# Layer-3 blocks among layer-2 values, and the eigenvectors' end moved to the end of the scores

## Chip, cores and metric

The kernel runs on one core of one Trainium2 chip. The metric is the time of one execution on the device, in microseconds (us). Before the change the median of three runs is 2519.87 us (2519.52 to 2521.8).

## The reference

The input x holds 128 graphs of 64 nodes with 256 features in float32; all graphs share one 64 x 64 adjacency matrix. Four layers follow one another, each as `x = layernorm(x + layer(x))`:

- Layer 0: two graph convolutions with relu, then four LSTMs over windows of 1, 2, 3 and 4 nodes.
- Layer 1: a normalized graph convolution with two linear maps and batch norms.
- Layer 2: attention over 512 edges with 4 heads. Scores of edges, a softmax over the edges that share a source node, a weighted sum of the values, an output map.
- Layer 3: the eigenvectors of the graph's Laplacian as a basis.

```python
# layer 2 (src, dst: the edges; A0 the adjacency)
e = einsum('behd,hd->beh', leaky_relu(Xq[:, src] + Xq[:, dst], 0.2), a)
e = e + log(A0[src, dst] + EPS)
attn = softmax of e over the edges of one src
Y = segment_sum(attn * Xv[:, dst], src);  return Y @ W_out.T
# layer 3
_, U = eigh(L_norm)
h = relu(einsum('mn,bnd->bmd', U.T, x) @ W1 + b1)
return einsum('nm,bmd->bnd', U, h @ W2 + b2)
```

## The kernel before

Two graphs make 128 partitions, so x is a tile X of 128 partitions x 64 tiles x 256 features that stays in SBUF through all layers. Each layer works on its tiles in turn. A norm (`Norm`, line 1218) adds a layer's result to X (line 1231), takes statistics of each tile (1234, 1235), and for a group of tiles forms the inverse root (`inv_sqrt`, line 1206) and rescales X on ScalarE (1252).

**The eigenvectors** depend on the adjacency alone. Their computation (`FastEigh.steps`) is a generator named `pieces`, a long chain of small VectorE operations with a few TensorE products. `pump(n)` issues pieces worth n units of work between the instructions of other layers. Its last part, the merge to 64, finds each eigenvalue by 31 bisection steps (mid, den, its reciprocal, a dot product, a comparison), and then builds the vectors. In before.py what is left of it is issued by `for _ in pieces` at the start of layer 3 (line 2021). Then `again` is computed and read into a register, and a loop of 0 or 1 turns (line 2030) runs a general method if the fast one failed. For these inputs it is not entered. After it, bdu and bdut (two copies of U and of its transpose on the diagonal) are filled.

**Layer 2** is a set of generators, advanced by `run(...)` in an order written out by hand (lines 1982 to 1998):

- `scores` (line 1848), 32 steps of one pair of tiles: transposes of X (1830), maps to queries and values (1841), a store of the values to DRAM (xv, 1845), then in two parts the edge sums (l, 1864), a copy and a leaky relu (xs, 1870 and 1871) and the products with the head vector (sc, 1817). Steps 0 to 15 are half 0, 16 to 31 half 1. Each step ends with `pump(work[0])`.
- `softmax` of a half (line 1885): scans over sorted edges, on VectorE and ScalarE.
- `table` (1905) transposes a half's weights and scatters them by edge into a DRAM table (attn_d) with four indirect DMAs on GpSimd's queue. `fetch` (1920) reads the table back as dense matrices M2 by eight DMAs of 512 KB on SP's queue; each is cut into pieces of 64 floats, since a half has two M2 tiles of 64 columns.
- `values` (1955), 33 steps: `load` copies eight columns of M2 into mc (ScalarE, 1934) and fetches xr (GpSimd's queue, 1937), `mixed` multiplies them (1949) and copies the product to yT (1952, one half of it on VectorE, one on ScalarE), and one step later the output map (1971) goes into the norm.

In the hand-written order four values steps run among the scores of half 1; after the scores come the rest of the values, with softmax, table and fetch of half 1 among them.

**Layer 3** follows in blocks of four tiles, each in four stages that are one block apart: `basis` (2059), `first_map` (2069), `back` (2077), `second_map` (2086), the norm and the store to the output. GpSimd adds a constant to X (2063).

The Tile scheduler sets each engine's final order from the program's order and estimated times, and may move an instruction ahead of earlier ones on its engine, even ahead of the loop; every engine then takes its own queue in order.

Of the kernel before, what the change touches and what calls it, by code (L numbers as in the profile page):

```python
# [7 lines left out]
F32 = mybir.dt.float32  # L8
I32 = mybir.dt.int32
AF = mybir.ActivationFunctionType  # L10
# [1195 lines left out]
def inv_sqrt(nc, pool, o, h):  # L1206

    s = pool.tile(list(h.shape), F32, tag="is_s", name="is_s")
    r = pool.tile(list(h.shape), F32, tag="is_r", name="is_r")
    nc.scalar.activation(s, h, AF.Sqrt)  # L1210
    nc.vector.reciprocal(r, s)  # L1211
    nc.vector.tensor_tensor(r, r, h, ALU.mult)
    nc.vector.tensor_tensor(r, r, s, ALU.add)
    nc.vector.reciprocal(r, r)
    nc.vector.tensor_scalar(o, r, 2.0, None, ALU.mult)


class Norm:
# [21 lines left out]
    def flush(self):  # L1240
        nc, n = self.nc, len(self.todo)
        v = self.pool.tile([P, self.n], F32, tag="ln_v", name="ln_v")
        rs = self.pool.tile([P, self.n], F32, tag="ln_rs", name="ln_rs")
        nc.vector.tensor_scalar(v[:, :n], self.mv[:, :n, 1], 1e-5, None, ALU.add)  # L1244
        inv_sqrt(nc, self.pool, rs[:, :n], v[:, :n])
        if self.act:
            sh = self.pool.tile([P, self.n], F32, tag="ln_sh", name="ln_sh")
            nc.vector.scalar_tensor_tensor(sh[:, :n], self.mv[:, :n, 0], -1.0, rs[:, :n], ALU.mult, ALU.mult)  # L1248
        for k, t in enumerate(self.todo):
            x = self.X[:, t, :]  # L1250
            if self.act:
                nc.scalar.activation(x, x, AF.Identity, bias=sh[:, k : k + 1], scale=rs[:, k : k + 1])  # L1252
                continue
            nc.vector.tensor_scalar(x, x, self.mv[:, k, 0:1], rs[:, k : k + 1], ALU.subtract, ALU.mult)
        self.todo = []
# [3 lines left out]
def tile_adj_resnorm(ctx: ExitStack, tc: tile.TileContext, I: dict, out: bass.AP, layers: int = 4):  # L1259
# [45 lines left out]
    bdu = const.tile([P, P], F32, tag="bdu", name="bdu")  # L1305
    bdut = const.tile([P, P], F32, tag="bdut", name="bdut")
# [7 lines left out]
    def col(tag):  # L1314
        return ek.tile([P, 1], F32, tag=tag, name=tag)
# [4 lines left out]
    cs_, deg, dg, jk = col("cs_"), col("deg"), col("dg"), ek.tile([P, P], F32, tag="jk", name="jk")  # L1320
# [8 lines left out]
    deg1, dinv, dv = col("deg1"), col("dinv"), ek.tile([P, P], F32, tag="dv_", name="dv_")  # L1329
# [19 lines left out]
    v.scalar_tensor_tensor(A, A, dinv[:N], dr, ALU.mult, ALU.mult)  # L1349
    U = ek.tile([P, N], F32, tag="U", name="U")  # L1350
# [417 lines left out]
    with tc.tile_pool(name="l2w", bufs=1) as lw, tc.tile_pool(name="l2s", bufs=2) as sm, tc.tile_pool(  # L1768
        name="l2p", bufs=2, space=PSUM
    ) as pp, tc.tile_pool(name="l2g", bufs=2, space=PSUM) as pg, tc.tile_pool(  # L1770
        name="l2c", bufs=2, space=PSUM
    ) as pc, tc.tile_pool(name="l2d", bufs=1, space=bass.MemoryType.DRAM) as dl:
# [51 lines left out]
        def transposed(k):  # L1824

            xT = []
            for t in (2 * k, 2 * k + 1):
                ps = pp.tile([P, 512], F32, tag="m", name="m")
                for c in range(2):
                    te.transpose(ps[:, c * P : (c + 1) * P], X[:, t, c * P : (c + 1) * P], ident)  # L1830
                xT.append(sm.tile([P, 2, P], F32, tag="xT", name="xT"))
                v.tensor_copy(xT[-1].rearrange("p c n -> p (c n)"), ps[:, :D])  # L1832
            return xT

        def maps(k, xT):

            xq, xv = [], sm.tile([P, 2, D], F32, tag="xv", name="xv")
            for i in range(2):
                ps = pp.tile([P, 512], F32, tag="m", name="m")
                for c in range(2):  # L1840
                    te.matmul(ps, xT[i][:, c, :], wqv[:, c, :], start=(c == 0), stop=(c == 1))  # L1841
                xq.append(sm.tile([P, D], F32, tag="xq", name="xq", bufs=4))
                taken.append(s.copy(xq[i], ps[:, :D]))  # L1843
                s.copy(xv[:, i, :], ps[:, D:])
            nc.sync.dma_start(xvd[k], xv)
            return xq

        def scores():
# [8 lines left out]
            for k in range(K):  # L1857
                xn = None
                for c in range(2):
# [8 lines left out]
                    for b, i in four:  # L1868
                        x = xs[b, i] = sm.tile([P, E], F32, tag="xs", name="xs", bufs=7)
# [15 lines left out]
        def softmax(half, es):  # L1885
# [5 lines left out]
            for c, e in enumerate(es):  # L1891
                f = sm.tile([P, E], F32, tag="sf", name="sf", bufs=1)
# [12 lines left out]
        def table(es):  # L1905

            at = sm.tile([P, 4, 2, HU, 2, 4], F32, tag="at", name="at", bufs=1)
            pt = pg.tile([P, 2, 512], F32, tag="l", name="l")
            for c, e in enumerate(es):
                ps = pt[:, c, :]  # L1910
# [9 lines left out]
        def fetch(half):  # L1920

            M2[half] = [lw.tile([P, N, N], F32, tag="M2", name="M2", bufs=3) for _ in range(2)]
            for k in range(2):
                for n0 in range(0, N, 32):
                    for b in range(2):
                        q = b * P + k * N
                        nc.sync.dma_start(
                            M2[half][k][b * N : (b + 1) * N, n0 : n0 + 32, :],
                            attn_d[: N * N, q : q + N].rearrange("(d n) q -> d n q", n=N)[:, n0 : n0 + 32, :])

        def load(k):
# [3 lines left out]
                   M2[half][u_ // 8][:, :, u_ % 8 * 8 : u_ % 8 * 8 + 8].rearrange("p n q -> p q n"))  # L1935
            x = sm.tile([P, 2, D], F32, tag="xr", name="xr")
# [3 lines left out]
        def mixed(m, x):  # L1940

            yT = sm.tile([P, 2, 2, P], F32, tag="yT", name="yT")
            for b in range(2):
# [8 lines left out]
                (s.copy if b else v.tensor_copy)(yT[:, :, :, r], py[:, :D].rearrange("p (i c n) -> p i c n", i=2, c=2))  # L1952
            return yT

        def values():
# [3 lines left out]
            for k in range(K + 1):  # L1959
# [6 lines left out]
                if k:  # L1966
                    po = (pg.tile([P, 2, 512], F32, tag="l", name="l")[:, 0, :] if alone[0] else
                          pp.tile([P, 512], F32, tag="m", name="m"))
# [10 lines left out]
        alone = [False]  # L1979
# [7 lines left out]
        work[0] = 3.5  # L1987
# [4 lines left out]
        run(sc_, sc_, sc_, *[sc_, sc_, val] * 4)  # L1992
        alone[0] = True
        run(val, soft[1], val, soft[1], soft[1], val, soft[1], val, soft[1], soft[1], val)
        table(es[1])
        run(val)
        fetch(1)
        run(*[val] * (NT // 2))
    if layers == 3:
        return finish()  # L2000

    with tc.tile_pool(name="l3w", bufs=1) as lw:
        w1 = lw.tile([P, 2, P], F32, tag="w31", name="w31")
        nc.sync.dma_start(w1, kio(I["W31"]))
        w2 = lw.tile([P, D], F32, tag="w32", name="w32")
        nc.sync.dma_start(w2, I["W32"])
        b1 = lw.tile([P, 1], F32, tag="b31", name="b31")  # L2010
        nc.sync.dma_start(b1, I["b31"])
        nb1 = lw.tile([P, P], F32, tag="nb1", name="nb1")
        nc.sync.dma_start(nb1, I["b31"].rearrange("p o -> (p o)").partition_broadcast(P))
        cb = lw.tile([P, D], F32, tag="cb", name="cb")
        nc.sync.dma_start(cb, I["b32"].partition_broadcast(P).rearrange("p o d -> p (o d)"))
        v.tensor_scalar(nb1, nb1, -1.0, None, ALU.mult)


        with tc.tile_pool(name="eps3", bufs=1, space=PSUM) as eps:
# [3 lines left out]
            ps = psum(P, D)  # L2023
            te.matmul(ps, b1.to_broadcast([P, P]), w2, start=True, stop=True)
            v.tensor_tensor(cb, cb, ps, ALU.add)
# [3 lines left out]
            v.tensor_scalar(again, ps, 0.0, None, ALU.is_gt)  # L2029
            with tc.For_i(0, nc.values_load(again[0:1, 0:1], min_val=0, max_val=1)):  # L2030
                with tc.tile_pool(name="gk2", bufs=1) as gk2, tc.tile_pool(name="gt2", bufs=2) as gt2, tc.tile_pool(
# [3 lines left out]
            for bd, m in ((bdu, U), (bdut, UT)):  # L2035
                v.memset(bd, 0.0)
                for b in range(2):
                    r = slice(b * N, (b + 1) * N)
                    v.tensor_copy(bd[r, r], m[r, :])  # L2039
            ps = psum(P, 1)  # L2040
            te.matmul(ps, bdut, ones[:, 0:1], start=True, stop=True)  # L2041
            ru = lw.tile([P, 1], F32, tag="ru", name="ru")
            v.tensor_copy(ru, ps)
            v.tensor_scalar(cb, cb, ru, None, ALU.mult)


        with tc.tile_pool(name="l3s", bufs=2) as sm, tc.tile_pool(name="l3p", bufs=8, space=PSUM) as pp:
            ln = Norm(nc, sm, X, 4, act=True)
            ov = out.rearrange("(t b) n d -> (b n) t d", b=2)
            bank = lambda: pp.tile([P, 512], F32, tag="ps", name="ps")  # L2050
# [3 lines left out]
            def basis(q):  # L2054
                ag[q] = sm.tile([P, 2, 512], F32, tag="ag", name="ag")
# [9 lines left out]
            def first_map(q):  # L2065
# [5 lines left out]
                h[q] = sm.tile([P, 4, P], F32, tag="h3", name="h3")  # L2071
                v.tensor_tensor(h[q], four(ps), nb1[:, None, :].to_broadcast([P, 4, P]), ALU.max)

            def back(q):
# [3 lines left out]
                uh[q] = sm.tile([P, 4, P], F32, tag="uh", name="uh")  # L2078
                s.copy(uh[q], four(ps))  # L2079

            def second_map(q):
                a = uh.pop(q)
                for j in range(0, 4, 2):
# [3 lines left out]
                    ln.add(q * 4 + j, ps, 2)  # L2087
                nc.sync.dma_start(ov[:, q * 4 : q * 4 + 4, :], X[:, q * 4 : q * 4 + 4, :])

            NQ = NT // 4  # L2090
            for q in range(NQ + 3):
                for k, stage in enumerate((basis, first_map, back, second_map)):
                    if 0 <= q - k < NQ:
                        stage(q - k)
# [62 lines left out]
```

## Time and profile before

| | us |
|---|---|
| median of three runs | 2519.87 |
| the profiled execution | 2520.43 |
| its span, first to last instruction | 2518.3 |
| TensorE busy in it | 2323.5 |
| VectorE busy in it | 1801.0 |
| ScalarE busy in it | 950.9 |
| GpSimd busy in it | 74.5 |

Times of the trace count from the start of the span. "Busy" is the time in which an engine works on at least one instruction; PE is TensorE, DVE VectorE, ACT ScalarE, POOL GpSimd and SP the queue that issues most DMAs. The clock given for TensorE is a share of its full clock. A matmul in float32 appears as two records, so x8 records are four matmuls of the program. Where a line ends in brackets, they hold the engine's idle time just before and what ended it.

### The profile page before, as it was taken

What the parts mean: (1) busy time and instruction counts of PE and PEld (TensorE: products, weight loads), DVE (VectorE), ACT (ScalarE), POOL (GpSimd) and SP (SyncE); (2) the same over time, 40 slices, a digit from 0 to 9 for tenths busy, and PEclk for the clock granted to TensorE, in tenths of its full rate; (3) what the DMA queues carried; (4) which work ended last, traced back from release to release, by engine and by line L of the source; (5) the groups of instructions that cost most, each with busy time, mean ns of one, the idle gap of its engine ahead of it and who ended that gap; (6) DMA issues with size and microseconds to landing.
All of it is one profiled execution on the core that took longest, in us unless ns stands there. A gap on an engine that the chain in (4) does not pass through costs nothing. (4 is left out here: it accounts for less than half of the span.)

```text
span 2518.3 us, 29398 instructions
## 1 busy us (share of the span) xinstructions
PE 2323.5 (92%) x9016; PEld 1239.4 (49%) x9016; DVE 1801.0 (72%) x8304; ACT 950.9 (38%) x1606; POOL 74.5 (3%) x115
## 2 busy tenths in 40 slices
PE   7999999999999999999999988989769988885787
PEld 5445655445655446644456434544323323344587
DVE  4666555676576798666897676879867787679857
ACT  1332222333222433322433212334465555455545
POOL 0000000000000000000000000000000000001142
PEclk9999999999999999999999988999769999997889
DMA  6000000001000101000010001022010006017212
GB/s 209 17 17 34 1 34 0 34 34 51 1 34 1 51 17 50 34 1 34 34 51 1 17 0 51 1 101 76 26 47 26 26 26 97 26 38 114 63 43 94
DMA packets 76244, 101.25 MB, mean 40 GB/s; under 512 B 37904, under 2 KB 56464, under 8 KB 75824
## 3 DMA queue, kind: packets, MB, share of 16 engines
q1 hardware_dynamic: 70688, 88.39, 11.6%
q0 software_dynamic: 3216, 10.21, 1.4%
q8 instruction: 72, 1.18, 0.2%
q10 hardware_dynamic: 2176, 0.72, 0.1%
q14 instruction: 92, 0.75, 0.1%
HBM read 67.84 MB, written 31.46 MB: 39 GB/s over the span
## 5 line engine op out<-in xcount | busy, mean ns | idle before, releaser
L1580 PE MATMUL pq<-H,wi 128*128 128x512 f32 (+1 forms) x2016 | 830.0, 547 | 3.8 <-DVE H L1605 3.8
L1586 ACT ACTIVATE gate<-pq,bl 128x512 f32<-128x512 f32 (+1 forms) x504 | 318.6, 635 | 845.4 <-PE pq L1584 658.3
L1580 PEld LDWEIGHTS pq<-H,wi 128*128 128x128 f32 x2016 | 370.6, 190 | 321.9 <-issue 252.2
L1584 PE MATMUL pq<-lh,wh 128*128 128x512 f32 (+1 forms) x1152 | 464.8, 531 | 5.3 <-DVE lh L1601 4.5
L1584 PEld LDWEIGHTS pq<-lh,wh 128*128 128x128 f32 x1152 | 215.2, 190 | 206.2 <-issue 141.1
L1871 DVE SCALAR_TENSOR_TENSOR xs<-xs 128x512 f32<-128x512 f32 x256 | 164.1, 678 | 57.8 <-ACT xs L1870 57.6
L1870 ACT COPY xs<-l 128x512 f32<-128x512 f32 x256 | 137.9, 592 | 103.7 <-PE l L1864 58.2
L1864 PE MATMUL l<-edge_s,xq 64*128 64x512 f32 x512 | 133.8, 617 | 9.8 <-ACT xq L1843 8.4
L1841 PE MATMUL m<-wqv,xT 128*128 128x512 f32 x256 | 129.9, 638 | 8.9 <-DVE xT L1832 8.9
L142 DVE COPY AQR<-eps 64x192 f32<-64x192 f32 (+1 forms) x125 | 35.1, 280 | 134.7 <-PE eps L148 134.7
L1725 PE MATMUL ps<-at,w 128*128 128x512 f32 x256 | 116.0, 607 | 8.6 <-DMA w<-in_W1T_dram 6.9
L1742 PE MATMUL ps<-h,w 128*128 128x512 f32 x256 | 112.7, 603 | 7.9 <-ACT h L1737 7.9
L1252 ACT ACTIVATE X<-X,ln_sh,ln_rs 128x256 f32<-128x256 f32 x192 | 98.5, 588 | 47.8 <-DVE ln_sh L1248 46.3
L1598 ACT ACTIVATE gate<-lc 128x1024 f32<-128x1024 f32 (+1 forms) x72 | 69.0, 958 | 89.0 <-DVE lc L1593 43.4
L1234 DVE BATCH_NORM_STATS2 ln_st<-X 128x6 f32<-128x256 f32 x256 | 99.9, 414 | 1.0
L1742 PEld LDWEIGHTS ps<-h,w 128*128 128x128 f32 x256 | 49.5, 194 | 71.0 <-issue 59.2
L1841 PEld LDWEIGHTS m<-wqv,xT 128*128 128x128 f32 x256 | 46.9, 201 | 73.2 <-issue 61.1
L1725 PEld LDWEIGHTS ps<-at,w 128*128 128x128 f32 x256 | 48.1, 193 | 66.5 <-issue 58.0
L1937 POOL DMA_DIRECT2D xr<-xv x32 | 17.4, 544 | 2122.2 <-ACT xs L1870 1872.0
L1864 PEld LDWEIGHTS l<-edge_s,xq 64*128 64x128 f32 x512 | 45.1, 186 | 68.7 <-issue 29.3
L1595 DVE TENSOR_TENSOR gate<-gate 128x1024 f32<-128x1024 f32 (+1 forms) x36 | 38.1, 1058 | 57.1 <-ACT gate L1586 56.8
L1817 PE MATMUL sc<-xs,az 128*32 128x512 f32 x512 | 69.7, 617 | 7.3 <-DVE xs L1871 7.3
(570 smaller groups left out, 3278.0 us busy)
## 6 DMA issues: line engine op xcount, KB each, us to landing
wi<-in_WihT_dram SPq DMA_DIRECT2D x16, 1024.0 KB, 4.8
wh<-in_WhhT_dram SPq DMA_DIRECT2D x12, 1024.0 KB, 7.3
X<-in_x_dram SPq DMA_DIRECT2D x16, 512.0 KB, 8.5
xd<-X SPq DMA_DIRECT2D x16, 512.0 KB, 2.6
X<-xd SPq DMA_DIRECT2D x16, 512.0 KB, 3.2
xv<-xv SPq DMA_DIRECT2D x32, 256.0 KB, 2.0
xr<-xv POOLq DMA_DIRECT2D x32, 256.0 KB, 2.9
M<-attn_d SPq DMA_DIRECT2D x16, 512.0 KB, 10.3
```

The source lines that it names most:

```text
L1234: nc.vector.bn_stats(st, self.X[:, k, :])
L1252: nc.scalar.activation(x, x, AF.Identity, bias=sh[:, k : k + 1], scale=rs[:, k : k + 1])
L1580: te.matmul(ps, wi[:, kk, o * P : (o + 1) * P], at(kk, k), start=(kk == 0), stop=(k == 0 and kk == 1))
L1584: te.matmul(ps, wh[:, kk, o * P : (o + 1) * P], hst[:, kk, :M], start=False, stop=(kk == 1))
L1586: s.activation(gates[gt][:, c, :M], ps, AF.Tanh if gt == 2 else AF.Sigmoid, bias=bl[:, p - 1, o : o + 1])
L1725: te.matmul(ps, w1[:, k, c * P : (c + 1) * P], at[:, k, :], start=(k == 0), stop=(k == 1))
L1742: te.matmul(ps, w2[:, k, c * P : (c + 1) * P], h[:, k, :], start=(k == 0), stop=(k == 3))
L1817: mms.append(te.matmul(sc[half][c][q : q + 32, :], az[:, c, HU - 1 - u_ : 3 * HU - 1 - u_], xs[b, i], start=(u_ == 0), stop=(u_ == HU - 1)))
L1841: te.matmul(ps, xT[i][:, c, :], wqv[:, c, :], start=(c == 0), stop=(c == 1))
L1864: mms.append(te.matmul(pl[i][:, b, :], xq[i][r, c * P : (c + 1) * P], GG[r, :], start=True, stop=True))
L1870: taken.append(s.copy(x, pl[i][:, b, :]))
L1871: ready.append(v.scalar_tensor_tensor(x, x, 0.2, x, ALU.mult, ALU.max))
```

## The change

- After 32 scores steps, of which two (before four) carry a values step among them, the scores' pools are closed, and the rest of `pieces`, `again`, bdu and bdut, and the loop come there. bdu and bdut use the storage of bda and bdah.
- `pump` gets 4.5 in place of 3.5 in the scores of half 1.
- After the loop: values of half 0 with softmax, table and fetch of half 1 among them, then 15 values steps with 10 of layer 3's block steps among them, then 2 values steps and the other layer-3 steps. The output map of the values takes its PSUM from layer 3's six banks.
- A half's M2 is one tile of 128 columns, fetched by eight DMAs of 512 KB in pieces of 128 floats.
- Both yT copies run on ScalarE. xs has 6 buffers (before 7), xr 3 (before 2). The softmax's scratch and the table share a buffer, and the table's transposes use the bank pair m.
- `inv_sqrt` takes the epsilon and folds two constants into other operations; it has one VectorE operation fewer.

```diff
-def inv_sqrt(nc, pool, o, h):
+def inv_sqrt(nc, pool, o, h, eps=0.0):
...
-    nc.scalar.activation(s, h, AF.Sqrt)
+    if eps:
+        t = pool.tile(list(h.shape), F32, tag="is_t", name="is_t")
+        nc.vector.tensor_scalar(t, h, eps, None, ALU.add)
+        h = t
+    nc.scalar.activation(s, h, AF.Sqrt, scale=0.25)
     nc.vector.reciprocal(r, s)
     nc.vector.tensor_tensor(r, r, h, ALU.mult)
-    nc.vector.tensor_tensor(r, r, s, ALU.add)
-    nc.vector.reciprocal(r, r)
-    nc.vector.tensor_scalar(o, r, 2.0, None, ALU.mult)
+    nc.vector.scalar_tensor_tensor(r, r, 0.25, s, ALU.mult, ALU.add)
+    nc.vector.reciprocal(o, r)
...
-    bdu = const.tile([P, P], F32, tag="bdu", name="bdu")
-    bdut = const.tile([P, P], F32, tag="bdut", name="bdut")
+    bdu, bdut = bda, bdah
...
-                        x = xs[b, i] = sm.tile([P, E], F32, tag="xs", name="xs", bufs=7)
+                        x = xs[b, i] = sx.tile([P, E], F32, tag="xs", name="xs", bufs=6)
...
-            M2[half] = [lw.tile([P, N, N], F32, tag="M2", name="M2", bufs=3) for _ in range(2)]
-            for k in range(2):
-                for n0 in range(0, N, 32):
-                    for b in range(2):
-                        q = b * P + k * N
-                        nc.sync.dma_start(
-                            M2[half][k][b * N : (b + 1) * N, n0 : n0 + 32, :],
-                            attn_d[: N * N, q : q + N].rearrange("(d n) q -> d n q", n=N)[:, n0 : n0 + 32, :])
+            M2[half] = lw.tile([P, N, P], F32, tag="M2", name="M2", bufs=2)
+            for n0 in range(0, N, 16):
+                for b in range(2):
+                    nc.sync.dma_start(
+                        M2[half][b * N : (b + 1) * N, n0 : n0 + 16, :],
+                        attn_d[: N * N, b * P : (b + 1) * P].rearrange("(d n) q -> d n q", n=N)[:, n0 : n0 + 16, :])
...
-                (s.copy if b else v.tensor_copy)(yT[:, :, :, r], py[:, :D].rearrange("p (i c n) -> p i c n", i=2, c=2))
+                s.copy(yT[:, :, :, r], py[:, :D].rearrange("p (i c n) -> p i c n", i=2, c=2))
...
-        work[0] = 3.5
+        work[0] = 4.5
         run(sc_)
         table(es[0])
         run(sc_)
         fetch(0)
-        run(sc_, sc_, sc_, *[sc_, sc_, val] * 4)
-        alone[0] = True
-        run(val, soft[1], val, soft[1], soft[1], val, soft[1], val, soft[1], soft[1], val)
-        table(es[1])
-        run(val)
-        fetch(1)
-        run(*[val] * (NT // 2))
...
+        run(*[sc_] * 7)
+        run(sc_, val, sc_, sc_, val, sc_)
+        scoring.close()
...
             for _ in pieces:
                 pass
...
             v.tensor_scalar(again, ps, 0.0, None, ALU.is_gt)
+            for bd in (bdu, bdut):
+                v.memset(bd, 0.0)
+            spread()
             with tc.For_i(0, nc.values_load(again[0:1, 0:1], min_val=0, max_val=1)):
...
+            l3 = blocks()
+            run(val, soft[1], val, soft[1], soft[1], val, soft[1], val, soft[1], soft[1], val)
+            table(es[1])
+            run(val)
+            constants()
+            run(val)
+            fetch(1)
+            run(*[val] * 7)
+
+            run(*[val, val, l3, val, l3] * 5)
+            run(*[val] * 2, *[l3] * (NT // 4))
```

`blocks` is the former loop over layer 3's blocks as a generator that yields after each turn; `constants` forms layer 3's constant from its bias rows, as the lines at the start of layer 3 did before.

## The prediction

> **What bounds the kernel now.** I read the forty slices first, then a cut of the span into stages, then single lines where a stage has idle.
>
> ```profile
> PE   7999999999999999999999988989769988885787
> PEclk9999999999999999999999988999769999997889
> ```
>
> TensorE (PE) is full up to layer 2, so only the last quarter can change by much. Stages there (columns: stretch, its length, busy time and count of each engine, TensorE clock, DMA share, GB/s):
>
> ```profile
> core 0: us, PE busy (x) PEld busy (x) DVE busy (x) ACT busy (x) POOL busy (x), PEclk, DMA share, GB/s
> 2134.00:2168.00 34.00, 23.47 (x87) 8.52 (x87) 17.66 (x74) 10.63 (x25) 0.00 (x0) 0.85 0.06 24
> 2168.00:2247.00 79.00, 74.02 (x450) 30.33 (x442) 59.63 (x205) 43.32 (x87) 2.76 (x5) 1.00 0.10 34
> 2247.00:2301.00 54.00, 45.99 (x468) 34.76 (x468) 48.35 (x159) 31.66 (x54) 10.00 (x15) 0.81 0.24 70
> 2301.00:2327.00 26.00, 1.61 (x32) 1.42 (x32) 23.34 (x118) 7.62 (x13) 0.54 (x1) 0.57 1.35 162
> 2327.00:2378.00 51.00, 48.07 (x609) 38.51 (x609) 45.53 (x215) 31.23 (x60) 6.99 (x13) 0.92 0.24 69
> 2378.00:2403.70 25.70, 5.09 (x18) 2.93 (x17) 11.72 (x70) 4.10 (x9) 0.00 (x0) 0.60 0.07 21
> 2403.70:2499.50 95.80, 95.80 (x741) 93.00 (x742) 71.07 (x233) 52.83 (x108) 44.44 (x64) 0.98 0.19 67
> 2499.50:2518.30 18.80, 5.16 (x28) 4.31 (x26) 11.34 (x57) 9.17 (x20) 0.00 (x0) 0.77 0.31 112
> ```
>
> In order: the scores' last third (last score tile done by VectorE, DVE, at 2247.2); values of half 0 beside softmax 1; the fetch of half 1; values of half 1; the eigenvectors' end and the loop; layer 3, where TensorE never idles; the last norms. TensorE idles 24 us at the fetch (26.00 - 1.61) and 21 us at the eigenvectors' end. Single lines of the timeline give the prices:
>
> ```profile
> 2252.60 3.78 PE L1971 MATMUL l<-wo,yT 128*128 128x256 f32 x8
> ...
> 2316.42 0.15 DVE L124 TENSOR_SCALAR mid<-lo 64x1 int32<-64x1 int32 x1
> ...
> 2318.40 0.15 DVE L124 TENSOR_SCALAR mid<-lo 64x1 int32<-64x1 int32 x1
> ...
> 2341.66 1.99 PE L1971 MATMUL l<-wo,yT 128*128 128x256 f32 x8
> 2343.58 0.97 PE L1949 MATMUL m<-mc,xr 64*64 64x64 f32 x32
> 2344.49 1.99 PE L1971 MATMUL l<-wo,yT 128*128 128x256 f32 x8
> ...
> 2395.31 0.15 DVE L2029 TENSOR_SCALAR again<-eps 1x1 int32<-1x1 f32 x1 [0.28 <-PE eps L2028]
> 2401.97 0.39 DVE L2039 COPY bdu<-U 64x64 f32<-64x64 f32 x2 [6.51 <-issue]
> ```
>
> A values step costs TensorE 2344.49 - 2341.66 = 2.83 us (0.91 mixing, 1.92 output); after idle the output takes 3.78. One bisection step of the eigenvalue search alone costs DVE 1.98 us. The loop that isn't taken stops everything for 6.5 us. A layer-3 block is 99.0/16 = 6.19 us of TensorE (1.78 + 1.79 + 0.89 + 1.73 in the chain).
>
> **What the Trainium skill says.** "TensorE: Matmul & The Clock Gate", "What's actually happening": an idle array drops to half clock, and some 3.4 us of work bring it back. The trace agrees (3.78 against 1.99, PEclk 0.50 within the fetch). "DMA: Bandwidth & Descriptors", Specifications: pieces below 512 B don't reach line rate. The trace agrees on the low side: the fetch's 256 B pieces run at 159 GB/s, the input's 1 KB pieces at 324 to 420; 512 B pieces are not in it. "Runtime: NRT & Kernel Launch", "Instruction fetch mechanics": a taken branch out of the prefetched instructions waits for a fetch. The 6.5 us here fit, without showing the cause.
>
> **The change, part by part.** I take the order of instructions on each engine from the changed program, since it is fixed when that is built.
>
> *Scores (end 2247.2 before).* Two values steps go: one mixing and 2.5 outputs, 0.91 + 2.5 x 1.92 = 5.7 us of TensorE, and about 1 us of waits at them. The pump of 4.5 brings 5 of 25 bisection steps forward; interleaved they are some 1.3 us each, 6.5 us of DVE, about what the norms and yT copies that move out gave back (2.5 x 1.8 and 5 x 0.41), in a stage where DVE has 19 us idle: cost 0, up to +6.5 if it comes in lumps. The tail of the 32-merge stalls TensorE (10.5 us idle in 2134:2168) and still does, but now with four score tiles inside the chain: -3 (between +2 and -8). The next merge's setup comes denser: +1. The M2 copy for half 0, in ScalarE's (ACT) queue between score copies, now needs the whole fetch and not its first half. Fetch starts at 2103.9; a 256 B piece takes 25.8 ns per DMA engine, a 1 KB one some 45, so 512 B is put at 32 ns by a straight line: 4.19 MB in 16.4 us, plus 2 to land, 2122.3, and the copy is due at 2120.6. Behind it in ACT's queue wait the score copies, and for these the scores on TensorE: +2 (0 at double rate, +9 at the old one). One xs buffer fewer delays the third copy by some 0.6 us, behind it are 1 us of transposes and maps: 0 (to +5). The table's and the loop's changed buffers, and bdu and bdut in the storage of bda and bdah, add two DVE clears of 0.17 us where DVE has room: 0. Sum -6.7: **the last score tile at 2240.5**.
>
> *The eigenvectors' end.* Now it stands before any further work on TensorE: after the last score matmul its queue holds only the eigenvectors' products and the loop. Ahead of the loop DVE has softmax 1 (eight scans of 1.21, two reciprocals of 3.34, five passes of 0.68, overlapped by 0.07: 18.8), three bisection steps among it (3.9), 17 alone (17 x 1.97 = 33.5), the end chain (delta to UT, bd copies, again: 15.7 from the lines after 2378 without the norms between them) and the loop, 6.5. Before, 25 steps and this softmax ran beside TensorE's values; that cover is gone. Sum 78.4: **the loop is left at 2318.9**. This is the largest term and is known to some 4 us. The old stop of 21 idle us at 2378 goes; what is late there next is layer 3's work itself.
>
> *Values of half 0.* Mixing 0 to 3 and output 0 are done. Two cold outputs 6.8, twelve steps at 3.0 = 36, table transposes and ACT's loads 3: 46 us. Steps are put above 2.83 because both yT copies are now ACT's: two steps are 4 x 0.27 + 2 x 0.98 + 1.97 + 0.15 = 5.2 of 5.66 us. Beside it: the table is on ACT at +18.5 (outputs 6.8, three steps 9.0, transposes 0.6, two copies 2.1); in POOL's queue its four scatters alternate with xr loads, the last behind mixing 9: +27, +1.0 issue, +2.6 landing; the fetch +16.4 +2, the M2 copy +1: **half 1 begins at +50.5, 2369.4**. Of the 26 us stop some 4.5 are left.
>
> *Half 1 with layer 3.* 16 x 2.83 + 16 x 6.19 = 144.3, 3 for the cold clock, 6 for losses in the mixing of two chains in order (per three values steps and two blocks ACT has 3 x 2.7 + 2 x 3.9 = 16 of TensorE's 20.9 us; six PSUM banks serve blocks and outputs together, where layer 3 had eight; bounds 0 and 15): 153.3. Layer 3's five small loads sit ahead of the fetch on SP and land long before. The adds of X and cb share POOL with the xr loads, which have three buffers: 0.
> The last norms stay 18.8. The shorter inverse root saves one DVE operation per norm group, some 0.15 us in layer 1's eight groups: -1; elsewhere it is hidden by TensorE.
>
> End: 2240.5 + 78.4 + 50.5 + 153.3 + 18.8 - 1.0 = 2540.5, against 2518.3: +22.2 us. The profiled execution took 2520.43, 0.56 above the median 2519.87: 2520.43 + 22.2 - 0.56 = **2542**.
>
> **Rivals.** *The fetch does not speed up* (159 GB/s for 512 B as well): scores +7, half 1 +10, 2559. For it: DMA share 1.35 at that rate, a saturated queue; against: 1 KB pieces run over twice as fast.
> *ACT sets the values' pace.* If its waits for norms make a step 3.5 us: 12 x 0.5 + 16 x 0.67 = 17, 2559. For it: 5.2 of 5.66 us; against: with DVE free of bisection the norms' answers come sooner.
> *The scores end early, and time is equal or better.* The place is 2134:2168. If the denser interleaving takes the merge's stall away whole, the last score tile comes at 2229 (-11.5); if then the fetch is hidden (-4.5, and -3 of clock) and the mixing loses nothing (-6): 2517. With the rest at its best it decides from a score end of 2236 (2542 - 13.5 - 4 is the edge of no change); against it, the changed order still has two products of the chain back to back in TensorE's queue.
> That blocks do not interleave is excluded by the order of TensorE's queue.
>
> **How the numbers follow.** Forecast 0.62 (its own range 2530 to 2554), fetch 0.10, ACT 0.13, early scores 0.10, something else, slower, 0.05. The early case falls on both sides of the 0.2% (5 us) that a measurement here tells from no change: faster 0.05, same 0.07, slower 0.88. The range reaches from the forecast's edge towards the early case, 2520, to beyond both slow rivals, 2564.
>
> **What would show it.** A stretch of 70 to 85 us after the last score matmul with TensorE nearly idle and DVE full; the loop's gap at its end; half 0's last output followed by 0 to 10 us of wait for M2; layer-3 matmuls among values; some 150 us from there to the last matmul. I am wrong if TensorE has work in that first stretch, if the scores end below 2230, or if the time from the loop to the end differs from 222 us by over 15.

## The result and the profile after

| | before | after |
|---|---|---|
| median of four runs, us | 2520.41 (2519.52 to 2521.8) | 2535.19 (2533.44 to 2536.99) |
| span of the profiled execution, us | 2518.3 | 2534.8 |

The ratio after to before is 1.0058, with a 95% interval of 1.0041 to 1.0076: the change makes the kernel some 15 us slower. The prediction was 2542 with a range of 2520 to 2564.

The forty slices of the kernel after, TensorE's busy share and its granted clock:

```profile
PE   7999999999999999999999969989679997925797
PEclk9999999999999999999999979999779998966899
```

One deep hole (the 2 and the 5 behind it) replaces two shallower ones of before. The cut into stages of the kernel after: the fetch of half 0 among the scores, the 32-merge's end, the rest of the scores, the eigenvectors' end, the values of half 0, the wait for half 1's table, half 1 with layer 3, the last norms.

```profile
core 0: us, PE busy (x) PEld busy (x) DVE busy (x) ACT busy (x) POOL busy (x), PEclk, DMA share, GB/s
2096.70:2126.00 29.30, 18.22 (x82) 6.50 (x82) 14.30 (x42) 12.59 (x26) 0.00 (x0) 0.87 0.98 162
2126.00:2170.00 44.00, 38.08 (x145) 13.32 (x145) 29.06 (x114) 16.77 (x36) 0.00 (x0) 0.89 0.05 19
2170.00:2236.80 66.80, 61.82 (x382) 23.82 (x378) 57.27 (x197) 37.78 (x78) 2.22 (x4) 1.00 0.11 36
2236.80:2310.60 73.80, 4.47 (x21) 2.18 (x21) 62.00 (x232) 1.26 (x2) 0.00 (x0) 0.51 0.00 1
2310.60:2362.80 52.20, 47.88 (x516) 38.09 (x516) 30.18 (x115) 36.61 (x74) 10.53 (x16) 0.88 0.65 136
2362.80:2372.90 10.10, 0.00 (x0) 0.00 (x0) 2.75 (x13) 4.07 (x9) 0.00 (x0) 0.75 0.83 132
2372.90:2523.00 150.10, 148.51 (x1408) 135.92 (x1408) 109.30 (x377) 96.49 (x201) 51.61 (x77) 0.97 0.22 70
2523.00:2534.80 11.80, 0.00 (x0) 0.00 (x0) 4.53 (x25) 6.31 (x14) 0.00 (x0) 0.72 0.38 133
```

In the fourth row TensorE works 4.47 of 73.8 us while VectorE works 62.0: this is the uncovered stage, called so because no work of TensorE covers VectorE's. In the sixth TensorE does nothing and waits for a transfer (DMA share 0.83). In the seventh TensorE works 148.5 of 150.1 us. Single lines of the timeline, at the places that were shown of before (a copy out of M2, two steps of the search, the loop's far side with the cold outputs, two values steps, and the start of half 1; what stands in brackets is the idle time before and what ended it):

```profile
2122.53 2.00 ACT L1937 COPY mc<-M 128x512 f32<-128x512 f32 x2 [8.67 <-DMA xv<-xv]
...
2125.56 3.60 PE L1869 MATMUL l<-edge_s,xq 64*128 64x512 f32 x8 [10.59 <-ACT xs L1875]
...
2285.12 0.15 DVE L124 TENSOR_SCALAR mid<-lo 64x1 int32<-64x1 int32 x1
...
2287.09 0.15 DVE L124 TENSOR_SCALAR mid<-lo 64x1 int32<-64x1 int32 x1
...
2307.33 0.14 DVE L2012 TENSOR_SCALAR again<-eps 1x1 int32<-1x1 f32 x1
...
2310.62 6.65 PE L1973 MATMUL ps<-wo,yT 128*128 128x256 f32 x16 [3.51 <-issue]
...
2334.37 1.99 PE L1973 MATMUL ps<-wo,yT 128*128 128x256 f32 x8
...
2337.20 1.99 PE L1973 MATMUL ps<-wo,yT 128*128 128x256 f32 x8
...
2372.92 3.26 PE L1952 MATMUL m<-mc,xr 64*64 64x64 f32 x64 [10.16 <-ACT mc L1937]
```

The first two lines are a new stop among the scores: ScalarE stands 8.67 us in front of the copy of M2 and holds the score copies behind it, and TensorE stands 10.59 us for one of these. The releaser that the first line names, a store of xv, is the transfer that was issued right behind the fetch on the same queue. A step of the search is 1.97 us (1.98 before), a values step 2.83 us as before, the time from `again` to the first product behind the loop 3.3 us.

### The profile page after: what moved, and what is told of

Same layout as the page of the kernel before. It is cut to its first block, busy times and chain, and to the rows that moved or that the text cites. A ratio compares the mean times of both kernels' runs of the same rounds, so it can differ in the third digit from the quotient of the medians.

```text
span 2534.8 us, 29282 instructions
## 1 busy us (share of the span) xinstructions
PE 2312.6 (91%) x9016; PEld 1234.9 (49%) x9016; DVE 1800.7 (71%) x8220; ACT 954.0 (38%) x1635; POOL 74.5 (3%) x115
## 5 line engine op out<-in xcount | busy, mean ns | idle before, releaser
L1869 PE MATMUL l<-edge_s,xq 64*128 64x512 f32 x512 | 133.9, 629 | 21.3 <-ACT xs L1875 12.1
L1234 DVE TENSOR_TENSOR X<-ps,X 128x256 f32<-128x256 f32 (+1 forms) x127 | 68.1, 537 | 52.4 <-PE ps L1973 35.6
```

The lines of the kernel that those rows point to most:

```text
L1869: mms.append(te.matmul(pl[i][:, b, :], xq[i][r, c * P : (c + 1) * P], GG[r, :], start=True, stop=True))
```

## The experiments

Twelve kernels were run. Ratios are to the kernel before, run beside them on the same chip, so small differences between sessions fall out. The theory: the loss is the stage in which TensorE has nothing (73.8 us), together with two stops of some 10 us at the fetches; that layer 3 stands among the values is worth nothing by itself. The rivals: VectorE's sum of work sets the time wherever it stands; the mixing of values and blocks changes the time; the fetch whole is the faster fetch. Of the smaller parts of the change only the inverse root was run alone; the yT copies on ScalarE, the buffer counts and the shared storage were not.

### Blocks behind the values again

```diff
-            run(*[val] * 7)
-            run(*[val, val, l3, val, l3] * 5)
-            run(*[val] * 2, *[l3] * (NT // 4))
+            run(*[val] * 24)
+            run(*[l3] * (NT // 4 + 3))
```

> One part undone: layer 3's blocks all come after the last values step, not among half 1's; the eigenvectors' end and the loop stay at the scores' end. Theory (the cost is the 73.8 us after the last score tile in which TensorE has nothing; TensorE is full in half 1 with layer 3 whether the blocks are mixed or not, 16 x 2.83 + 16 x 6.19 us): 2535, between 2531 and 2541. Rival (the mixing saves time that values alone lose to waits of ScalarE and VectorE): 2545 or more.

Measured: 2536.46 us, ratio 1.0075 (1.0058 to 1.0092), inside the theory's range. The part of the change that its name puts first moves nothing that can be told from noise (1 us by the medians, 4 by the ratios, whose intervals overlap). TensorE is nearly full in both orders: from the start of half 1 to the last matmul it takes 151.7 us, with 4.0 of waits, against 150.1 with 1.6 in the kernel after. What cost the time is what had to happen first, the move of the eigenvectors' end.

### The fetch in two parts again

```diff
-            M2[half] = lw.tile([P, N, P], F32, tag="M2", name="M2", bufs=2)
+            M2[half] = [lw.tile([P, N, N], F32, tag="M2", name="M2", bufs=4) for _ in range(2)]
...
-                   M2[half][:, :, u_ * 8 : u_ * 8 + 8].rearrange("p n q -> p q n"))
+                   M2[half][u_ // 8][:, :, u_ % 8 * 8 : u_ % 8 * 8 + 8].rearrange("p n q -> p q n"))
```

with the fetch's loops of before.

> One part undone: the table is fetched as before in two parts of 64 columns (256 B pieces), each part a tile of its own, so that the first eight mixings of a half wait for the first part only. Theory (512 B pieces run at about the rate of 256 B ones, 173 against 159 GB/s, and a copy that waits for the whole table waits twice as long): the 10.6 us stop of TensorE among the scores goes or shrinks below 3 us, and so does the 10.2 us stop at the start of half 1: 2517, between 2512 and 2524. Rival (the fetch whole is the better one): some 2 us per fetch more, 2535 to 2541.

Measured: 2522.4 us, ratio 1.0012 (1.0005 to 1.0019), so 13 us less than after (12 by the ratios). TensorE's longest waits in the last fifth, first the kernel after, then this one (total, times, longest):

```profile
PE eps L183 <- DVE mid L117: 55.8, 1, 55.8
PE l L1869 <- ACT xs L1875: 12.1, 4, 10.6
PE m L1952 <- ACT mc L1937: 10.2, 1, 10.2
```

```profile
PE eps L183 <- DVE mid L117: 55.8, 1, 55.8
PE m L1954 <- ACT mc L1939: 6.7, 1, 6.7
...
PE l L1869 <- ACT xs L1875: 4.6, 5, 1.9
```

The uncovered stage stays (55.8). The stop among the scores is gone: they take 6.9 us less from first to last matmul, not 10.6. TensorE waits 7.5 us less for score copies, but 1.1 more for dg (a tile of VectorE's chain in the 32-merge; mid, S, V and delta below are such tiles too) and 1.4 more for xv; it idles 4.8 us less in all and is busy 2.1 us less. The wait at half 1 only shrank, from 10.2 to 6.7, and the time from the loop's exit to half 1 from 62.3 to 56.3; the fetch runs beside the xr loads there, which may be why its first part too came late. The theory holds, with 6.9 + 6.0 us in place of 10 + 10.

### Half 0's values ahead of the loop

```diff
         scoring.close()
+        run(val, soft[1], val, soft[1], soft[1], val, soft[1], val, soft[1], soft[1], val)
+        table(es[1])
+        run(val, val)
+        fetch(1)
+        run(*[val] * 7)
...
-            run(val, soft[1], val, soft[1], soft[1], val, soft[1], val, soft[1], soft[1], val)
-            table(es[1])
-            run(val)
             constants()
-            run(val)
-            fetch(1)
-            run(*[val] * 7)
```

> One move undone: half 0's values with softmax 1, the table and the fetch of half 1 are put ahead of the eigenvectors' end and the loop; layer 3 stays among half 1's values. Theory (uncovered stage): the search's last steps run beside half 0's values, the fetch beside both; VectorE has 18.8 (softmax) + some 35 (20 steps) + 15.7 + 28 (14 norms) = 97 us to the loop instead of 73.8, but 62 us between the loop and half 1 go: 2535 - 62 + 24 + 3 = 2500, between 2490 and 2512. Rival (VectorE's sum of softmax, search and norms sets the time wherever it stands): 2530 to 2540.

Measured: 2500.5 us, ratio 0.9928 (0.9912 to 0.9945). This one move takes 35 us off the kernel after (33 by the ratios) and beats the kernel before. The stages from the last score tile on (values of half 0 beside softmax and search, the eigenvectors' end and the loop, half 1 with layer 3, the last norms):

```profile
2233.00:2315.00 82.00, 53.63 (x552) 40.87 (x544) 71.81 (x288) 46.49 (x84) 11.09 (x17) 0.78 0.49 100
2315.00:2336.30 21.30, 5.71 (x52) 3.90 (x52) 10.00 (x56) 2.73 (x4) 1.07 (x2) 0.50 0.16 43
2336.30:2484.60 148.30, 146.73 (x1356) 134.34 (x1356) 112.34 (x392) 94.94 (x201) 50.55 (x75) 0.99 0.22 68
2484.60:2496.40 11.80, 0.00 (x0) 0.00 (x0) 4.53 (x25) 6.30 (x14) 0.00 (x0) 0.72 0.38 134
```

82.0 + 21.3 = 103.3 us stand between the scores and the stage in which TensorE is full, where the kernel after has 73.8 + 52.2 + 10.1 = 136.1. TensorE works 53.6 us in the first of them. The rival (VectorE's sum) is out as an account of the kernel after; but here VectorE works 71.8 of 82 us, and looks like the next bound. Against the kernel before, this trace is 21.9 us shorter in three places: 8.9 ahead of the scores (in part spread, see the inverse root below), 5.5 in the scores and 7.4 behind them.

### More of the search among the scores

```diff
-        work[0] = 4.5
+        work[0] = 8.5
```

> One number changed: the pump of the second half's scores from 4.5 to 8.5, so that all of the eigenvalue search and the eigenvectors' end stand among the score tiles; softmax 1 alone and the loop are left after them. Theory (uncovered stage; VectorE has 40 us idle among these scores): after the last score tile 25 us instead of 73.8, the scores 20 us longer at most: 2507, between 2492 and 2516. Rival (a step among the scores delays them by as much as it saves behind them): 2530 to 2540.

Measured: 2518.57 us, ratio 0.9995 (0.9987 to 1.0004): better than after, but outside what I gave for the theory, and no better than before. Its stages (the scores behind the fetch; softmax, the eigenvectors' end and the loop; values of half 0):

```profile
2122.00:2260.00 138.00, 113.23 (x497) 41.41 (x497) 115.78 (x433) 59.20 (x124) 1.14 (x2) 0.90 0.06 22
2260.00:2291.40 31.40, 4.24 (x28) 2.38 (x20) 26.66 (x68) 2.32 (x3) 0.00 (x0) 0.50 0.01 2
2291.40:2342.00 50.60, 46.80 (x570) 37.63 (x570) 29.82 (x115) 38.30 (x79) 11.61 (x18) 0.92 0.63 140
```

The uncovered stage shrinks from 73.8 to 31.4 us, and the scores end 22 us later (last score matmul at 2259.0, at 2236.8 in the kernel after, with the first at the same time). About half of what is saved comes back: TensorE has 113 of 138 us of work there and VectorE 116, and score products and the merge's products wait in one queue for VectorE's chain (6.1 us for mid before score products, 4.9 for S and 3.1 for mid before products of the merge). The edit also did less than I expected of it: all 31 search steps stand among the scores, but the eigenvectors' end does not. It runs between the passes of softmax 1, and TensorE waits 15.7 us for dg and 8.7 for V in that second stage. Here idle time in a stage was not room for as much work.

### The shorter inverse root alone

In the kernel before, `inv_sqrt` and its call as in the kernel after.

> The kernel before with one part of the change alone: the shorter inverse root (one VectorE operation fewer for each group of norms, and its last multiplication gone). In the trace after, the scores start 5.4 us earlier than before, 3.3 us of it gained while layer 1's last norms run, where I had reckoned 1. Theory (the shorter chain counts in those norms): 2519.5 - 4 = 2515.5, between 2513.5 and 2517.5. Rival (the 5.4 us are mostly the spread between executions): 2518.5 to 2520.

Measured: 2517.78 us, ratio 0.9992 (0.9984 to 1.0001): -2.4 us with an uncertainty of as much. It falls between theory and rival, and does not decide. The scores' first matmul comes 4.8 us earlier in its trace than in that of before, but among the kernels with the shorter root it comes anywhere from 1863.7 to 1868.9, so part of the 5.4 us is spread.

### Both causes undone, and the loads

> Two parts undone together: half 0's values and the fetch ahead of the eigenvectors' end (as in the run that measured 2500.5), and the table fetched in two parts of 64 columns (as in the run that measured 2522.4, 13 us less than after). Theory (two causes that add): 2500.5 - 13 = 2487, between 2482 and 2493. Rival (with the values ahead, VectorE's work up to the loop sets half 1's start, and only the stop among the scores counts): 2494 or more.

Measured: 2493.68 us, ratio 0.9894 (0.9879 to 0.9909). The number falls between the two ranges; the trace speaks for the rival. The scores take 6.3 us less than in the run of 2500.5, of 6.8 in the time. TensorE's wait for half 1's table shrinks from 8.5 to 3.9 us as well, but the time from the last score tile to the first product behind the loop stays (103.4 us for 103.6): TensorE waits for VectorE's chain there (5.0 us for delta, 3.6 for V, 2.8 for dg).

> The run before it with layer 3's five small loads ahead of the loop instead of behind it. With the values ahead of the loop, TensorE waited 7.4 us for the last of these loads after the loop. Theory: these 7 us go: 2480, between 2475 and 2486. Rival (the layer-3 products that follow wait for something else as late, the loop's own exit or the norms): within 2 of the run before it.

```diff
+        hold = ExitStack()
+        l3w = hold.enter_context(tc.tile_pool(name="l3w", bufs=1))
+        w1 = l3w.tile([P, 2, P], F32, tag="w31", name="w31")
+        nc.sync.dma_start(w1, kio(I["W31"]))
...
         with tc.tile_pool(name="eps3", bufs=1, space=PSUM) as eps:
```

Measured: 2490.06 us, ratio 0.9878 (0.9863 to 0.9894), the lowest median of all, though its interval overlaps that of the run before it. Neither case came: TensorE's wait of 7.2 us became one of 3.5 that is the loop's own, so half of it went. VectorE's gap at the same loop is longer:

```profile
2330.43 1.22 PE L2054 MATMUL ps<-w,b 128*128 128x256 f32 x2 [3.51 <-issue]
...
2332.97 0.16 DVE L2057 COPY ru<-ps 128x1 f32<-128x1 f32 x1 [5.69 <-issue]
```

### What sets the fetch's rate

Four kernels ask for the cause of the term that I had wrong by most. Their tables and transfers differ thus:

| table and transfers | bytes in one run | partitions of a transfer | GB/s |
|---|---|---|---|
| before | 256 | 64 | 163 |
| after | 512 | 64 | 185 |
| fewer partitions | 512 | 32 | 188 |
| two tensors | 8192 | 64 | 219 |
| order of partitions | 4096 | 128 | 378 |
| the same, transfers halved | 4096 | 64 | 237 |

The rates are means of all traffic over the middle of a fetch: of the one among the scores, of before that of half 1. The 173 of the expectations is the commonest single slice of the kernel after; over the whole of that fetch, 4.19 MB in 24.8 us, it is 169.

```diff
-    attn_d = dram.tile([N * N + E, 2 * P], F32, tag="attn_d", name="attn_d")
+    attn_d = [dram.tile([N * N + E, P], F32, tag=f"attn_d{b}", name="attn_d") for b in range(2)]
```

> The kernel after with the table kept as two tensors of 128 columns, written by eight scatters of 512 B rows instead of four of 1 KB rows, so that what a fetch reads for a partition lies in one run (8 KB for each transfer). It tells what sets the fetch's 173 GB/s. Theory (short pieces): above 300 GB/s, 4.19 MB in 14 us or less, both stops of 10 us shrink below 3: 2535 - 15 = 2520, between 2513 and 2527. Rival (the reading of 4.19 MB into 128 partitions, not the pieces): rate and time unchanged, 2533 to 2540.

Measured: 2530.32 us, ratio 1.0043 (1.0028 to 1.0058). Between both cases: the rate rises by a fifth only; the stops are 8.5 and 11.8 us (10.6 and 10.2 in the kernel after).

> The kernel after with the same 512 B pieces and the same eight transfers for a fetch, but each transfer cut so that it fills 32 partitions with 32 pieces each instead of 64 partitions with 16. Keeping each fetch piece in one 8 KB run raised the rate from 173 to 216 GB/s only, well below the 380 to 420 of the input's transfers, which fill all 128 partitions. Theory (the number of partitions that one transfer fills sets its rate): about half of 173, a fetch of 45 us, both stops of TensorE 16 to 20 longer: 2568, between 2552 and 2585. Rival (partitions don't matter, what is read does): 173 GB/s and 2532 to 2540.

Measured: 2532.21 us, ratio 1.0049 (1.0032 to 1.0066), and no loss of rate, as the rival said. The theory failed for short pieces: half the partitions, the same rate.

```diff
-    attn_d = dram.tile([N * N + E, 2 * P], F32, tag="attn_d", name="attn_d")
+    attn_d = dram.tile([3 * N * N + E, P], F32, tag="attn_d", name="attn_d")
...
+                    M2[half][:, n0 : n0 + 8, :],
+                    attn_d[: 2 * N * N, :].rearrange("(d n) q -> d n q", n=N)[:, n0 : n0 + 8, :])
```

> The other way: the table is one tensor in which the second graph's rows follow the first's, so that a transfer fills all 128 partitions with 4 KB each (eight scatters of 512 B rows with a second set of row numbers). Against the run with 8 KB runs into 64 partitions (216 GB/s, 2530.3) only the partitions of a transfer and the length of a run differ. Theory (partitions of a transfer): 330 GB/s or more, a fetch in 13 us; the stop among the scores goes from 8.5 to below 3, that at half 1 from 11.8 to 4: 2518, between 2511 and 2524. Rival (216 GB/s is what such writes give): 2527 to 2534.

> The run with the table in the order of the partitions (4 KB runs, 128 partitions for each transfer, 400 GB/s), with each transfer cut in two, one for each half of the partitions; the runs, the scatters and everything else stay. Theory (the 64 partitions of a transfer are what made 216 GB/s of 400): a rate near 216 and a fetch of about 20 us instead of 11. Rival (the length of the runs, 4 KB against 8 KB): the rate stays above 350. The time is not what is asked; either way within 2528 to 2546.

Measured: 2530.14 us, ratio 1.0041 (1.0027 to 1.0055), and with halved transfers 2529.63, ratio 1.0037 (1.0021 to 1.0053). The rates of 40 slices from 2345 to 2375 us, where half 1's table is fetched, first with 128 partitions to a transfer, then with 64:

```profile
GB/s 55 246 49 87 0 164 219 66 0 131 339 333 339 306 328 273 339 333 344 382 361 415 388 410 421 421 322 115 38 0 0 0 0 0 0 60 235 71 147 186
```

```profile
GB/s 66 246 268 273 295 208 262 229 273 268 257 257 240 235 240 257 251 224 246 246 251 257 235 229 240 208 66 11 0 0 0 0 0 0 120 229 109 240 0 22
```

Up to 421 against some 240, as the theory of the halved transfers said. Halving also made the transfers smaller (256 KB in place of 512), but the run with two tensors has 512 KB transfers and 219 GB/s; what the two slow kernels share is the 64 partitions. So for long runs these held the rate down, as far as these runs tell. And still neither run gained over the one with two tensors (2530.3): with 128 partitions the theory's rate came and the rival's time. What the faster fetch gave went into the scatters before it. Two of the eight, from GpSimd's queue:

```profile
2087.19 1.00 POOL L1924 DMA_INDIRECT attn_d<-at,edge_s  x1 [1.53 <-DMA attn_d<-at,edge_s]
2089.72 0.97 POOL L1924 DMA_INDIRECT attn_d<-at,edge_s  x1 [1.53 <-DMA attn_d<-at,edge_s]
```

Each waits for the one before to land, both writing one tensor: 2.5 us apiece, eight of them, and the fetch starts at 2105.7 instead of 2096.7, and 39.9 us behind the loop instead of 30.5. With two tensors pairs overlap (1.6 us apiece on average), but there the rate is 219.

The slower fetch of the halved transfers cost no time, and the traces show why: half 0's first copy out of M2 has another place in ScalarE's queue, which the scheduler chose. It stands behind 182 score copies in the kernel after, with the fetch in two parts and with two tensors, and behind 180 with 128 partitions; but behind 188 with halved transfers and 196 with fewer partitions. First with 128 partitions, then with halved transfers:

```profile
2120.96 2.01 ACT L1939 COPY mc<-M 128x512 f32<-128x512 f32 x2 [10.15 <-DMA M<-attn_d]
```

```profile
2128.95 2.04 ACT L1941 COPY mc<-M 128x512 f32<-128x512 f32 x2 [7.52 <-DMA xv<-xv]
```

In the second ScalarE waits where the 32-merge makes TensorE wait too (5.1 us for dg), and TensorE's longest wait for a score copy is 0.8 us in place of 11.0. The scores took 359.3 us for 371.5, and the stop at half 1 16.3 us for 11.3. With fewer partitions the two stops were 1.1 and 15.9. So the times of these two runs don't follow from their rates, and the stop among the scores can go without a faster fetch; no run moved the copy alone.

> Half 0's values and layer 3's loads ahead of the loop, as in the run of 2490.1, with the table in the order of the run before instead of fetched in two parts. Theory (partitions of a transfer): half 1's table is there before VectorE is through with the search, the 3.9 us wait for it goes: 2486, between 2481 and 2492. Rival (rate unchanged): the stop among the scores comes back, 2494 or more.

Measured: 2499.53 us, ratio 0.9922 (0.9905 to 0.9938). The rival's number, but with the faster fetch: the late scatters bring back an 11.3 us stop among the scores, and TensorE's wait for half 1's table, which was to go, is 7.7 us.

## Why the prediction was right, and where it was not

The sign, the mechanism and the largest term were right; the end was 5.7 us too high (2540.5 against 2534.8), and that is small only by luck, because errors of +11.8 and -10.2 us cancel (5.2 of the latter is work that my sum holds twice, see half 1).

| step | predicted | measured |
|---|---|---|
| ahead of the scores (inverse root) | -1 | -5.4, part of it spread |
| the scores themselves | -6.7 | -5.0 (369.5 for 374.5 us) |
| last score tile to the loop's exit | 78.4 | 73.8 |
| loop's exit to half 1 | 50.5 | 62.3 |
| half 1 with layer 3, and the last norms | 172.1 | 161.9 |

**Scores.** The sum is near and its terms are not. From first to last matmul TensorE's busy time falls from 345.8 to 338.1 us, 7.8 less (5.7 predicted). Its idle time rises by only 2.7, though the wait for the whole fetch(0), put at +2 (0 to +9), was a stop of 10.6: so 7.9 us of other waits went, more than the 4 put for them, 4.6 of it at the 32-merge (10.5 us idle in 2134:2168 of before, 5.9 in 2126:2170 of after). That is the early-scores rival's mechanism, and the late table is why it did not show as time: with the fetch in two parts the scores took 362.6 us, 11.9 less than before, where the rival had 11.5.

**The eigenvectors' end.** Softmax and three steps took 22.6 us (22.7), the 17 steps 33.6 (33.5). Mis-sized were the end chain, 14.3 us for 15.7, and the loop, 3.3 for 6.5. The 6.5 were VectorE's gap, and not everything's as I had it: before, the copies of U stood behind the loop, and TensorE waited for them. In the kernel after they stand ahead of it, and TensorE's own gap counts. From the end of `again` to TensorE's next instruction it was 3.1 to 3.2 us in all nine kernels in which that instruction waited for nothing else; VectorE's was 5.7 to 9.0 in the three that show it free of other waits.

**Half 0 and the fetch.** The table was through ScalarE at +18.6 (18.5), and the fetch was issued at +30.5 (30.6; with the terms behind it the sum gives 50.0, not 50.5). The term that failed is the fetch, "16.4 us, plus 2 to land", from 32 ns for a piece of 512 B, a straight line between 256 B and 1 KB pieces. It took 30.7 us to the first copy beside the xr loads, 25.8 among the scores. The rate rose from 163 to 185 GB/s (the means of the table), where my straight line wanted 256 (4.19 MB in 16.4 us). So my first rival, no faster fetch, was nearly true. Its price of 7 + 10 us above the forecast compares with 8.6 among the scores (a stop of 10.6 where I had put 2) and 11.8 up to half 1; its total of 2559 did not come, since other terms were lower. The Trainium skill ("DMA: Bandwidth & Descriptors", Specifications) puts the least size for line rate at 512 B; here 512 B pieces did not reach it with 64 partitions to a transfer: they ran at 185 GB/s, half the rate of 4 KB runs into 128 partitions (378), but not so far below 4 and 8 KB runs into 64 (237 and 219). The line was drawn between pieces that filled 64 partitions (256 B) and pieces that filled 128 (1 KB); two things differed, and I saw one. With 64 partitions to a transfer the length of the piece was worth a fifth to a quarter of the rate; 512 B pieces into 128 partitions were not tried.

The ScalarE rival is out: values steps run at 2.83 us, TensorE's own pace. Only the last of half 0 are slower, beside the fetch (one waits 2.3 us for its xr load).

**Half 1 with layer 3.** My sum holds 5.2 us twice: 16 blocks of 6.19 us are all of layer 3's work, and the 18.8 us of the last norms, kept as they were, hold its last 5.16 us of TensorE again. Without that my terms give 153.3 us to the last matmul, and 150.1 were measured: 5.8 above the bare work of 144.3, where I had put 9. TensorE idles 1.6 us in all, so of the 6 us of mixing loss little was there; it is busy 4.2 us more than the bare work, which fits the 3 for the cold clock (the first output of half 1 takes 3.78 us, a warm one 1.99). The last norms end 11.8 us after the last matmul, 13.6 before.

## What to carry to other kernels

Before a step is moved, ask what work covered it where it was. Here a VectorE chain of 74 us stood alone, with 62 us of values and fetch behind it; put beside them, all took 103 us in place of 136 (2500.5). The mixing for which it had been moved changed nothing that the runs can tell: two streams that each fill the same engine gained nothing by it. A transfer into one tile makes its first reader wait for all of it; with the same table in two tiles the stop among the scores went from 10.6 us to under 2 and that at half 1 from 10.2 to 6.7. And a price read from one engine's gap, as that of the loop, holds for that engine only.

## What the runs showed of the hardware

- For runs of 4 KB, transfers into 128 partitions moved 378 GB/s and the same transfers cut into two of 64 partitions 237; runs of 8 KB into 64 partitions 219. For 512 B pieces 64 and 32 partitions made no difference (185 and 188).
- Four or eight indirect writes into one tensor mostly followed one another at 2.5 to 2.9 us each (up to 3.8), of which 1.0 is issue and 1.5 to 1.9 the wait for the one before where nothing else stood between; into two tensors in turn, at 1.6 us on average.
- Behind a dynamic loop that is not entered, TensorE's next instruction came 3.1 to 3.2 us after the value that the loop reads (nine kernels), VectorE's 6.5 us after it in the kernel before, 9.0 in that with the shorter root alone, and 5.7 in the run of 2490.1 us. Why VectorE takes longer was not tried.
